# Attention with its projections in four column groups and its transposes in row tiles, ahead of a GRU

## The chip, the core and the metric

The kernel runs on one core of a Trainium2 chip. The core has five engines with instruction queues of their own: TensorE (PE, with its weight loads, PEld), VectorE (DVE), ScalarE (ACT), GpSimd (POOL) and SyncE (SP), which here only issues DMAs. The metric is the device time in microseconds (us) of one execution. All data are fp32.

## The reference

For each of 16 batches, with x of 256 tokens by 512 features and a condition vector `cond`:

```python
scale, shift = split(cond @ W_emb + b_emb)
xn = rms_norm(x, g_norm) * (1 + scale) + shift
q, k, v = split(xn @ W_qkv)              # 16 heads of 32
q, k = rms_norm(q, g_q), rms_norm(k, g_k)   # over the 32 of a head
o = softmax(q @ k.T * 32**-0.5) @ v
x = x + o + o @ W_out
h = cond                                    # GRU, 256 steps in sequence over t
gi, gh = x[:, t] @ W_ih + b_ih, h @ W_hh + b_hh    # each split into r, z, n
r, z = sigmoid(gi_r + gh_r), sigmoid(gi_z + gh_z)
n = tanh(gi_n + r * gh_n)
h = (1 - z) * n + z * h;  out[:, t] = x[:, t] + h
```

## The kernel before

The program has two halves. The first does the attention of all batches and keeps the heads' outputs on chip in `oT`. The second runs the GRU over 256 time steps; between its steps it computes the output projection and the input product of later steps. Only the first half and what leads into it is touched by the edit. The GRU's `product` (L648), which the edit leaves alone, already writes four column groups: four matmuls with 32 stationary columns each, to partitions 0, 32, 64 and 96 of one PSUM bank.

The loop over the attention (L579 to L586) has four slots per batch, one for each group of four heads. Slot g of batch b does two kinds of work. One is the attention of the group: logits (L300), the negated row maxima (`maxima`), exponentials with their sums (`exps`), and the division by the sums on GpSimd (`normalize`). The group before it, `prev`, goes on at the same time: its attention matrix is transposed (`turn`), copied out of PSUM (`put_turned`), multiplied with v (`weigh`) and copied to `oT` (`put_weighed`). The other kind prepares batch m = b + 1: its q, k and v projections for both halves n of the tokens (`project`), the norm of q and k (`Stats`, `norm_qk`), their transposes (`turn_qk`) and the copies of these to `qT` and `kT`. The x of later batches is normed too: batch b + 3's is squared in slot 2 and scaled in slot 3, and in slot 0 the x of batch b + 2 is transposed (`turn_x`) and written with scale and shift to `xnT` (`put_x`).

A projection of 128 tokens to 512 outputs takes four steps, one for each 128 features k; a step is one fp32 matmul of 128 stationary columns and 512 moving columns, which the machine runs as two issues. The 24 steps of a batch are spread over the four slots. Where a projection is begun in one slot and ended later, its accumulator stays in PSUM. There are eight PSUM banks: lg0 to lg3 hold the logits and, once the exponentials are done, the transposes of the group before; A, X, Y and Z go from one use to the next.

Transposes go through TensorE: the data are the stationary operand and the identity is the moving one. Those of x, q and k take a whole 128x128 block in one issue. The attention's, in `turn`, take two row tiles of 64 partitions, R and QR in the code, each of which writes its own bank, so that `put_turned` puts the interleaved halves back.

The order on TensorE, VectorE, ScalarE and GpSimd is the order in which the code is written (`manual_schedule`); there is no planner. An engine waits for the operand of its next instruction and everything behind it waits too. The lines of the profile that matter are L242 (projection), L310 (logits), L361 (transposes of the attention), L282 and L221 (transposes of q, k and of x), L385 (weighing), L325 (maxima), L331 (exponentials), L233 and L231 (copies of x), L287 and L292 (copies of q and k), L375 (copies of the attention), L262 (copy of v), L268 (norm of q and k).

The last batch has four short slots (`slot_last`), without work for a next batch. Ahead of the loop, the x of the first batches and all of batch 0's projections are done.

Of the kernel before, what the change touches and what calls it, by code (L numbers as in the profile page):

```python
# [9 lines left out]
AF = mybir.ActivationFunctionType  # L10
ALU = mybir.AluOpType
AX = mybir.AxisListType
PSUM = bass.MemoryType.PSUM

P = 128
# [4 lines left out]
def kernel(  # L20
# [17 lines left out]
    nc = tc.nc  # L38
# [3 lines left out]
    KC = D // P  # L42
# [119 lines left out]
    def tile_ps(name, bank, shape=(P, D)):  # L162
        pool = ps if len(bank) == 1 else ps_lg
        return pool.tile(list(shape), F32, tag=bank, name=name)
# [48 lines left out]
        if 0 < b and b + 2 < B:  # L213
            load_x(b + 2)

    def turn_x(b, half, bank):
        tp = tile_ps(f"tpx_{b}_{half}", bank, (P, 2, T))
        for cc in range(2):
            c = 2 * half + cc
            for n in range(NT):  # L220
                nc.tensor.transpose(  # L221
                    tp[:, cc, n * P : (n + 1) * P], batches[b].xs[:, n, c * P : (c + 1) * P], ident
                )
        return tp

    def put_x(b, half, tp, engine=nc.vector):
        for cc in range(2):
            c = 2 * half + cc
            a, s = ada_a[:, c, b : b + 1], ada_s[:, c, b : b + 1]
            if engine is nc.scalar:  # L230
                nc.scalar.activation(batches[b].xnT[:, c, :], tp[:, cc, :], AF.Identity, bias=s, scale=a)  # L231
            else:
                nc.vector.tensor_scalar(  # L233
                    batches[b].xnT[:, c, :], tp[:, cc, :], a, s, ALU.mult, ALU.add
                )

    def project(b, n, s, ks, a):

        if isinstance(a, str):
            a = tile_ps(f"qkv_{b}_{n}_{s}", a)  # L240
        for k in ks:
            nc.tensor.matmul(  # L242
                a,
                batches[b].xnT[:, k, n * P : (n + 1) * P],
                wq[:, k, s * D : (s + 1) * D],
                start=(k == 0),
                stop=(k == KC - 1),
            )
        return a

    def square(b, n, s, a):
# [23 lines left out]
        return out  # L275

    def turn_qk(b, n, normed, banks):
        tps = []
        for s in range(2):
            tp = tile_ps(f"tpqk_{b}_{n}_{s}", banks[s], (P, NG, P))  # L280
            for c in range(NG):
                nc.tensor.transpose(tp[:, c, :], normed[s][:, c * P : (c + 1) * P], ident)  # L282
            tps.append(tp)
        return tps

    def put_q(n, tps):
        nc.vector.tensor_scalar(qT[:, :, n * P : (n + 1) * P], tps[0], gq_col, None, ALU.mult)  # L287

    def put_k(n, tps, engine=nc.scalar):
        dst = kT[:, :, n * P : (n + 1) * P]  # L290
        if engine is nc.scalar:
            nc.scalar.activation(dst, tps[1], AF.Copy, scale=gk_col)  # L292
        else:
            nc.vector.tensor_scalar(dst, tps[1], gk_col, None, ALU.mult)


    class Group:
# [24 lines left out]

    def maxima(w, heads):
        for i in heads:
            nc.vector.tensor_reduce(w.neg[:, i, :], w.lg[i], AX.X, ALU.max, negate=True)  # L325

    def exps(w, heads):
        for i in heads:
# [8 lines left out]
    def normalize(w, heads=range(HG), engine=nc.gpsimd):  # L337
        r = slice(heads[0], heads[-1] + 1)
        nc.vector.reciprocal(w.rden[:, r, :], w.den[:, r, :])  # L339
        for i in heads:  # L340
            for n in range(NT):
# [2 lines left out]
                    ALU.mult, ALU.mult,  # L344
                )

    R, QR = 2, P // 2

    def turn(w, banks=("lg0", "lg1", "lg2", "lg3")):

        if w is None:
            return
        w.tp = [tile_ps(f"tpa_{w.b}_{w.g}_{i}", banks[i], (P, R, NT, NT, QR)) for i in range(HG)]
        for i in range(HG):
            for n in range(NT):
                for k in range(NT):
                    for r in range(R):
                        q = slice(QR * r, QR * r + QR)  # L360
                        nc.tensor.transpose(  # L361
                            w.tp[i // R * R + r][:, i % R, k, n, :],
                            w.attn[i][q, n, k * P : (k + 1) * P],
                            ident[q, q],
                        )
        w.attnT = p1.tile([P, HG, NT, T], F32, tag="attnT", name=f"attnT_{w.b}_{w.g}")

    def put_turned(w, engines):

        if w is None:  # L370
            return
        for i, e in enumerate(engines):
            h, r = i // R * R, i % R
            dst = w.attnT[:, h : h + R].rearrange("p h k (n r c) -> p h k n r c", n=NT, r=R)[:, :, :, :, r]
            (nc.scalar.copy if e == "a" else nc.vector.tensor_copy)(dst, w.tp[i])  # L375

    def weigh(w, bank):
        if w is None:
            return
        v = batches[w.b].v  # L380
        w.o = tile_ps(f"o_{w.b}_{w.g}", bank, (P, T))
        for k in range(NT):
            for i in range(HG):
                h = w.g * HG + i
                nc.tensor.matmul(  # L385
                    w.o[i * DH : (i + 1) * DH, :],
                    v[:, k, h * DH : (h + 1) * DH],
                    w.attnT[:, i, k, :],
                    start=(k == 0),
                    stop=(k == NT - 1),  # L390
                )
# [20 lines left out]
    def slot0(b, w, prev, st):  # L412
        m = b + 1
        if b == 0:
            rstd = batches[2].rs.second()
        maxima(w, range(HG))
        if b == 0:
            norm_apply(2, rstd)
        project(b, 1, 2, range(1 if b == 0 else 2, KC), st.v1)
        if b == 0:  # L420
            st.q = project(m, 0, 0, (0,), "A")
        if b + 2 < B:
            tpx = [turn_x(b + 2, half, "YZ"[half]) for half in range(2)]
        if b == 0:
            project(m, 0, 0, range(1, KC), st.q)
        else:
            st.q = project(m, 0, 0, (0, 1), "A")
        exps(w, range(HG))
        if b + 2 < B:
            for half in range(2):  # L430
                put_x(b + 2, half, tpx[half])
        put_v(b, 1, st.v1)
        turn(prev)
        put_turned(prev, "vava")
        if b > 0:
            project(m, 0, 0, (2, 3), st.q)
        normalize(w)
        weigh(prev, "Z")
        st.s0 = Stats(m, 0)
        st.sq = st.s0.square(0, st.q)  # L440
        put_weighed(prev)

    def slot1(b, w, prev, st):
        m = b + 1
        k = project(m, 0, 1, range(KC), "Y")
        st.q1 = project(m, 1, 0, (0, 1), "Z")
        maxima(w, range(HG))
        exps(w, range(HG))
        st.s0.add(0, st.sq)
        st.s0.add(1, st.s0.square(1, k))  # L450
        st.s0.rs.first()
        turn(prev)
        put_turned(prev, "vava")
        project(m, 1, 0, (2, 3), st.q1)
        rstd = st.s0.rs.second()
        weigh(prev, "X")
        normalize(w)
        st.qk0 = norm_qk(m, 0, (st.q, k), rstd)
        st.s1 = Stats(m, 1)
        st.sq = st.s1.square(0, st.q1)  # L460
        put_weighed(prev)
# [26 lines left out]
    def slot3(b, w, prev, st):  # L488
        m = b + 1
        last = m == B - 1  # L490
        tq0 = turn_qk(m, 0, st.qk0, "ZA")
        project(m, 0, 2, (2, 3), st.v0)
        st.v1 = project(m, 1, 2, (0, 1) if last else (0,), "X")
        maxima(w, range(HG))
        if b + 3 < B:
            rstd = batches[b + 3].rs.second()
        put_q(0, tq0)
        if b + 3 < B:
            norm_apply(b + 3, rstd)
        exps(w, range(HG))  # L500
        put_v(m, 0, st.v0)
        put_k(0, tq0)
        turn(prev)
        put_turned(prev, "vava")
        tq1 = turn_qk(m, 1, st.qk1, "ZA")
        project(m, 1, 2, (2, 3) if last else (1,), st.v1)
        put_q(1, tq1)
        put_k(1, tq1)
        normalize(w)
        weigh(prev, "Y")  # L510
        if last:
            put_v(m, 1, st.v1)
        put_weighed(prev)
# [17 lines left out]
    with tc.manual_schedule(engines=ORDERED):  # L531
# [9 lines left out]
        wih = wpool.tile([P, KC, 3 * D], F32, tag="w_a", name="wih")  # L541
        for k in range(KC):
            nc.sync.dma_start(wih[:, k, :], w_ih[k * P : (k + 1) * P, :])
        for half in range(2):
            put_x(0, half, turn_x(0, half, "AX"[half]))
        q = project(0, 0, 0, range(KC), "Y")
        k = project(0, 0, 1, range(KC), "Z")
        s0 = Stats(0, 0)
# [9 lines left out]
        norm_apply(1, batches[1].rs.second())  # L558
        k = project(0, 1, 1, range(KC), "X")
        tq = turn_qk(0, 0, qk, ("lg0", "lg1"))  # L560
        tpx = [turn_x(1, half, f"lg{2 + half}") for half in range(2)]
        v = project(0, 0, 2, range(KC), "Y")
        s1.add(1, s1.square(1, k))
        s1.rs.first()
        put_q(0, tq)
        put_k(0, tq, nc.vector)
        qk = norm_qk(0, 1, (q, k), s1.rs.second())
        for half in range(2):
            put_x(1, half, tpx[half], nc.scalar)
        norm_first(2)  # L570
        batches[2].rs.first()
        tq = turn_qk(0, 1, qk, "ZA")
        st.v1 = project(0, 1, 2, (0,), "X")
        put_q(1, tq)
        put_k(1, tq)
        put_v(0, 0, v)

        prev = None
# [286 lines left out]
```

## Time and profile before

| | us |
|---|---|
| median of three runs (1822.04 to 1822.92) | 1822.74 |
| profiled execution | 1822.2 |
| its span, first to last instruction | 1820.4 |
| TensorE busy in matmuls | 1754.8 |
| VectorE, ScalarE, GpSimd busy | 1114.5, 815.0, 316.2 |
| projection matmuls (L242) busy, 768 issues | 362.6 |
| transposes of attention, of q and k, of x busy | 88.3, 34.9, 17.7 |

A line of the timeline gives the start in us from the span's start, the length in us, the engine, the line of the kernel, the operation, out<-in by the program's names, the rows*columns of the array that the instruction uses, the shape, and the count of merged instructions; an idle time in brackets is that of the engine ahead of the instruction, with what ended it. A line of the groups gives busy time, mean ns of one instruction, and idle time ahead of it with what ended it. Since matmuls are pipelined, their lengths overlap; from one group of matmuls to the next the difference of the starts is what counts.

### The profile page before, as it was taken

To read this page: it belongs to the slowest core of one execution; us is meant where nothing else is said; L and a number is where in the kernel's file an instruction comes from. 1 tells how busy PE (TensorE), PEld (TensorE's weight loads), DVE (VectorE), ACT (ScalarE), POOL (GpSimd) and SP (SyncE) were. 2 spreads that over 40 slices of the span, in tenths; PEclk is the share of its full clock that TensorE was granted. 3 is DMA by queue.
4 is the path that set the end of the run, shared out by engine and by line. 5 is a ranking of instruction groups with operands and counts; after the bars stand their busy time and mean duration, and the time that the engine had idled before them with its cause. 6 is when DMAs were issued, how large, how long until landed. Compare 5 with 4: busy or idle time off the path is not lost.

```text
span 1820.4 us, 86417 instructions
## 1 busy us (share of the span) xinstructions
PE 1754.8 (96%) x38066; PEld 1237.9 (68%) x38066; DVE 1114.5 (61%) x3611; ACT 815.0 (45%) x2723; POOL 316.2 (17%) x769
## 2 busy tenths in 40 slices
PE   7999999999999889999999999999999999999975
PEld 3555555555555447887887887888888888888865
DVE  4666666666766635566566566566566565665555
ACT  3677777777777633333333333333333333333322
POOL 0434333433433320000000000000000000000000
PEclk9999999999999989999999999999999999999999
DMA  7200000000000110001101101100110100000000
GB/s 260 54 13 13 13 24 13 13 14 13 13 2 1 71 25 10 15 17 24 18 16 22 21 16 19 23 16 15 22 21 15 21 16 10 11 15 10 10 15 15
DMA packets 146200, 43.37 MB, mean 24 GB/s; under 512 B 137899, under 2 KB 138031, under 8 KB 145823
## 3 DMA queue, kind: packets, MB, share of 16 engines
q1 hardware_dynamic: 145287, 36.72, 8.8%
q8 instruction: 299, 4.90, 1.1%
q10 hardware_dynamic: 536, 1.12, 0.2%
q14 instruction: 78, 0.64, 0.1%
HBM read 29.41 MB, written 8.39 MB: 21 GB/s over the span
## 4 chain that ended last, share of the span: by engine, by line
PE 85%; DVE 6%; ACT 6%; issue 2%; DMA 1%; POOL 0%; ACTq 0%; DVEq 0%; POOLq 0%
PE gi L651 17%; PE qkv L242 14%; PE gr L713 13%; PE gn L713 12%; PE gz L713 11%; PE o L651 6%; ACT attn L331 5%; PE lg L310 4%; PE o L385 4%; PE tpa L361 3%; DVE neg L325 2%; DVE tr L725 1%; PE tpqk L282 1%; PE tpx L221 1%; DVE h L816 0%
## 5 line engine op out<-in xcount | busy, mean ns | idle before, releaser
L651 PE MATMUL gi<-xT,wih 128*32 128x256 f32 x6144 | 364.7, 379 | 0.0
L242 PE MATMUL qkv<-wq,xnT 128*128 128x512 f32 x768 | 362.6, 606 | 0.0
L342 POOL TENSOR_SCALAR attn<-attn,rden 128x256 f32<-128x256 f32 x508 | 233.5, 483 | 422.2 <-DVE rden L339 331.9
L713 PE MATMUL gr<-whh,h 128*16 128x128 f32 x8160 | 272.2, 274 | 25.1 <-DVE h L817 23.7
L713 PEld LDWEIGHTS gr<-whh,h 128*16 128x16 f32 x8160 | 200.5, 96 | 108.6 <-DVE h L817 108.6
L331 ACT ACTIVATE attn<-lg,neg 128x256 f32<-128x256 f32 x512 | 234.8, 485 | 82.0 <-DVE neg L325 47.8
L713 PE MATMUL gz<-whh,h 128*16 128x128 f32 x8160 | 269.5, 273 | 0.0
L713 PE MATMUL gn<-whh,h 128*16 128x128 f32 x8160 | 269.5, 273 | 0.0
L819 POOL TENSOR_TENSOR y<-xT,h 128x64 f32<-128x64 f32 x255 | 81.9, 321 | 1071.6 <-DVE h L817 1034.5
L651 PEld LDWEIGHTS gi<-xT,wih 128*32 128x32 f32 x6144 | 195.9, 110 | 100.9
L788 ACT ACTIVATE r<-r 128x64 f32<-128x64 f32 x256 | 65.7, 257 | 380.4 <-DVE r L787 380.4
L325 DVE TENSOR_REDUCE neg<-lg 128x2 f32<-128x512 f32 x256 | 158.9, 683 | 117.6 <-PE lg L310 116.5
L242 PEld LDWEIGHTS qkv<-wq,xnT 128*128 128x128 f32 x768 | 135.4, 190 | 137.5 <-issue 129.3
L725 DVE STREAM_TRANSPOSE tr<-gr 128x128 f32<-128x128 f32 x256 | 81.1, 317 | 237.1 <-PE gr L713 237.1
L713 PEld LDWEIGHTS gn<-whh,h 128*16 128x16 f32 x8160 | 224.7, 97 | 0.0
L713 PEld LDWEIGHTS gz<-whh,h 128*16 128x16 f32 x8160 | 224.7, 97 | 0.0
L695 ACT ACTIVATE gi<-gi,cols 128x256 f32<-128x256 f32 x192 | 91.2, 475 | 163.9 <-PE gi L651 163.9
L725 DVE STREAM_TRANSPOSE tr<-gn 128x128 f32<-128x128 f32 x256 | 81.1, 317 | 76.0 <-PE gn L713 76.0
L651 PE MATMUL o<-oT,wo 128*32 128x256 f32 x2048 | 121.7, 379 | 0.7 <-ACT oT L396 0.7
L361 PEld LDWEIGHTS tpa<-ident,attn 64*128 64x128 f32 x2048 | 75.1, 142 | 61.8 <-issue 45.1
L331 ACT ACTIVATION_READ_ACCUMULATOR attn<-lg,neg 128x1 f32 x512 | 111.0, 217 | 0.0
L794 ACT ACTIVATE n<-n 128x64 f32<-128x64 f32 x256 | 65.5, 256 | 98.5 <-DVE n L793 98.5
(98 smaller groups left out, 1720.8 us busy)
## 6 DMA issues: line engine op xcount, KB each, us to landing
x<-in_x_dram SPq DMA_DIRECT2D x16, 512.0 KB, 3.6
xin<-in_x_dram SPq DMA_DIRECT2D x256, 32.0 KB, 2.6
out_dram<-osb SPq DMA_DIRECT2D x248, 32.0 KB, 3.2
wq<-in_L_cond_W_qkv_dram SPq DMA_DIRECT2D x12, 256.0 KB, 4.2
wih<-in_L_cond_W_ih_dram SPq DMA_DIRECT2D x4, 768.0 KB, 10.9
whh<-in_L_cond_W_hh_dram SPq DMA_DIRECT2D x4, 768.0 KB, 5.7
we<-in_L_cond_W_emb_dram SPq DMA_DIRECT2D x2, 512.0 KB
we<-in_L_cond_W_emb_dram ACTq DMA_DIRECT2D x2, 512.0 KB, 6.5
```

What stands on the lines that cost most here:

```text
L242: nc.tensor.matmul(a, batches[b].xnT[:, k, n * P : (n + 1) * P], wq[:, k, s * D : (s + 1) * D], start=(k == 0), stop=(k == KC - 1),)
L310: nc.tensor.matmul(w.lg[i][:, n, :], qT[r, g, n * P : (n + 1) * P], kT[r, g, :], start=True, stop=True,)
L325: nc.vector.tensor_reduce(w.neg[:, i, :], w.lg[i], AX.X, ALU.max, negate=True)
L331: nc.scalar.activation(a[:, n, :], w.lg[i][:, n, :], AF.Exp, bias=w.neg[:, i, n : n + 1], accum_out=w.den[:, i, n : n + 1],)
L342: engine.tensor_scalar(w.attn[i][:, n, :], w.attn[i][:, n, :], w.rden[:, i, n : n + 1], 1.0, ALU.mult, ALU.mult,)
L361: nc.tensor.transpose(w.tp[i // R * R + r][:, i % R, k, n, :], w.attn[i][q, n, k * P : (k + 1) * P], ident[q, q],)
L385: nc.tensor.matmul(w.o[i * DH : (i + 1) * DH, :], v[:, k, h * DH : (h + 1) * DH], w.attnT[:, i, k, :], start=(k == 0), stop=(k == NT - 1),)
L651: nc.tensor.matmul(acc[32 * j : 32 * j + 32, :], w[:, k, m * P + 32 * j : m * P + 32 * j + 32], rhs, start=(k == 0), stop=(k == KC - 1),)
L695: nc.scalar.activation(gis[grp][:, m].rearrange("p t b -> p (t b)"), acc["i"], AF.Identity, bias=bcols[:, m : m + 1],)
L713: nc.tensor.matmul(gates[g][32 * j : 32 * j + B, :], hT[:, k, :], whh[:, k, g * D : (g + 1) * D].rearrange("p (q j c) -> p j q c", q=KC, c ...
L725: nc.vector.transpose(tr.rearrange("p q b -> p (q b)"), gates[g])
L819: (nc.gpsimd if t + 1 < T else nc.vector).tensor_tensor(y[:, :, tl * B : (tl + 1) * B], xTs[grp][:, :, ti, :], h, ALU.add)
```

## The change

- `project` writes four column groups: each step is four matmuls with 32 tokens as stationary columns, to the partitions 32j to 32j + 31 of the bank, all with the same 512 moving columns.
- `turn_block` takes over the two row tiles of `turn`, and `turn_x` and `turn_qk` use it as well. A tile of x or of q and k now holds one half r (64 of each 128 tokens), in one bank for each r; x's two banks hold all four feature chunks, and those of q and k hold both.
- `put_x` copies one half r with eight instructions in all of 128x128 for a batch (four of 128x256 before). `put_qk` takes the place of `put_q` and `put_k`: VectorE copies half 0 of q and of k, ScalarE half 1 of both, each 128x256 (before, VectorE copied q and ScalarE k, each 128x512).
- `maxima` reduces the first head in two instructions, one for each half n of the tokens; the other heads as before.
- The order in the slots: transposes of x stand right ahead of `turn` in slot 0; in slot 3 those of q and k stand right ahead of it and right behind it, and the projection steps ahead of and behind these. Slot 0 now has one step of batch b's v and, of batch m, four of q and one of k; slot 1 has seven steps, slot 2 six, slot 3 five. The weighing of slot 0 goes to bank X in place of Z. In slot 3 the norm of x is issued on VectorE ahead of the copies of q and k.
- Ahead of the loop the same helpers are used, with the copies of x of batch 0 dealt to VectorE and ScalarE.

```diff
+    R, QR = 2, P // 2
+    def turn_block(dst, src):
+        for r in range(R):
+            q = slice(QR * r, QR * r + QR)
+            nc.tensor.transpose(dst[r], src[q], ident[q, q])
+    def turn_x(b, banks):
+        tps = [tile_ps(f"tpx_{b}_{r}", banks[r], (P, KC, NT, QR)) for r in range(R)]
+        for c in range(KC):
             for n in range(NT):
-                nc.tensor.transpose(
-                    tp[:, cc, n * P : (n + 1) * P], batches[b].xs[:, n, c * P : (c + 1) * P], ident
+                turn_block(
+                    [tp[:, c, n, :] for tp in tps], batches[b].xs[:, n, c * P : (c + 1) * P]
                 )
+    def put_x(b, r, tps, chunks=range(KC), engine=nc.vector):
+        for c in chunks:
+            dst = batches[b].xnT[:, c, :].rearrange("p (n r q) -> p n r q", n=NT, r=R)[:, :, r]
...
         for k in ks:
-            nc.tensor.matmul(
-                a,
-                batches[b].xnT[:, k, n * P : (n + 1) * P],
-                wq[:, k, s * D : (s + 1) * D],
+            for j in range(4):
+                nc.tensor.matmul(
+                    a[32 * j : 32 * j + 32, :],
+                    batches[b].xnT[:, k, n * P + 32 * j : n * P + 32 * j + 32],
+                    wq[:, k, s * D : (s + 1) * D],
...
+        tps = [tile_ps(f"tpqk_{b}_{n}_{r}", banks[r], (P, 2, NG, QR)) for r in range(R)]
         for s in range(2):
             for c in range(NG):
-                nc.tensor.transpose(tp[:, c, :], normed[s][:, c * P : (c + 1) * P], ident)
+                turn_block([tp[:, s, c, :] for tp in tps], normed[s][:, c * P : (c + 1) * P])
+    def put_qk(n, r, tps, engine):
+        for s, (dst, g) in enumerate(((qT, gq_col), (kT, gk_col))):
+            dst = dst[:, :, n * P + QR * r : n * P + QR * r + QR]
+            if engine is nc.scalar:
+                nc.scalar.activation(dst, tps[r][:, s], AF.Copy, scale=g)
+            else:
+                nc.vector.tensor_scalar(dst, tps[r][:, s], g, None, ALU.mult)
...
         for i in heads:
-            nc.vector.tensor_reduce(w.neg[:, i, :], w.lg[i], AX.X, ALU.max, negate=True)
+            for n in (slice(0, 1), slice(1, 2)) if i == 0 else (slice(0, 2),):
+                nc.vector.tensor_reduce(
+                    w.neg[:, i, n], w.lg[i][:, n, :], AX.X, ALU.max, negate=True
+                )
...
@@ slot0 @@
+        project(b, 1, 2, range(1, KC) if b == 0 else (3,), st.v1)
+        before = 1 if b == 0 else 3
+        st.q = project(m, 0, 0, range(before), "A")
+        tpx = turn_x(b + 2, "YZ") if b + 2 < B else None
         exps(w, range(HG))
         put_v(b, 1, st.v1)
         turn(prev)
+        if tpx:
+            put_x(b + 2, 0, tpx)
         put_turned(prev, "vava")
+        if tpx:
+            put_x(b + 2, 1, tpx)
+        project(m, 0, 0, range(before, KC), st.q)
+        st.k = project(m, 0, 1, (0,), "Y")
         normalize(w)
-        weigh(prev, "Z")
+        weigh(prev, "X")
...
@@ slot1 @@
-        k = project(m, 0, 1, range(KC), "Y")
+        k = project(m, 0, 1, range(1, KC), st.k)
...
@@ slot3 @@
+        project(m, 0, 2, (2, 3), st.v0)
+        st.v1 = project(m, 1, 2, (0, 1), "X")
         tq0 = turn_qk(m, 0, st.qk0, "ZA")
-        project(m, 0, 2, (2, 3), st.v0)
-        st.v1 = project(m, 1, 2, (0, 1) if last else (0,), "X")
         maxima(w, range(HG))
...
-        put_q(0, tq0)
...
         put_v(m, 0, st.v0)
-        put_k(0, tq0)
+        put_qk(0, 0, tq0, nc.vector)
+        put_qk(0, 1, tq0, nc.scalar)
         turn(prev)
         put_turned(prev, "vava")
         tq1 = turn_qk(m, 1, st.qk1, "ZA")
-        project(m, 1, 2, (2, 3) if last else (1,), st.v1)
-        put_q(1, tq1)
-        put_k(1, tq1)
+        project(m, 1, 2, (2, 3) if last else (2,), st.v1)
+        put_qk(1, 0, tq1, nc.vector)
+        put_qk(1, 1, tq1, nc.scalar)
```

More of the change, by code (lines that the diff above doesn't have):

```diff
@@ L214, in norm_apply @@
             load_x(b + 2)
[L216 to L219, printed above, removed]
+    R, QR = 2, P // 2
[6 more added lines that the diff above has]
+        for c in range(KC):
             for n in range(NT):
-                nc.tensor.transpose(
-                    tp[:, cc, n * P : (n + 1) * P], batches[b].xs[:, n, c * P : (c + 1) * P], ident
-                )
[L224 to L228, printed above, removed]
+                turn_block(
+                    [tp[:, c, n, :] for tp in tps], batches[b].xs[:, n, c * P : (c + 1) * P]
+                )
+        return tps
+    def put_x(b, r, tps, chunks=range(KC), engine=nc.vector):
+        for c in chunks:
             a, s = ada_a[:, c, b : b + 1], ada_s[:, c, b : b + 1]
+            dst = batches[b].xnT[:, c, :].rearrange("p (n r q) -> p n r q", n=NT, r=R)[:, :, r]
             if engine is nc.scalar:
-                nc.scalar.activation(batches[b].xnT[:, c, :], tp[:, cc, :], AF.Identity, bias=s, scale=a)
+                nc.scalar.activation(dst, tps[r][:, c], AF.Identity, bias=s, scale=a)
             else:
-                nc.vector.tensor_scalar(
-                    batches[b].xnT[:, c, :], tp[:, cc, :], a, s, ALU.mult, ALU.add
-                )
+                nc.vector.tensor_scalar(dst, tps[r][:, c], a, s, ALU.mult, ALU.add)
     def project(b, n, s, ks, a):
@@ L241, in project @@
         for k in ks:
-            nc.tensor.matmul(
-                a,
-                batches[b].xnT[:, k, n * P : (n + 1) * P],
-                wq[:, k, s * D : (s + 1) * D],
-                start=(k == 0),
-                stop=(k == KC - 1),
-            )
+            for j in range(4):
[3 more added lines that the diff above has]
+                    wq[:, k, s * D : (s + 1) * D],
+                    start=(k == 0),
+                    stop=(k == KC - 1),
+                )
         return a
@@ L277, in turn_qk @@
     def turn_qk(b, n, normed, banks):
-        tps = []
+        tps = [tile_ps(f"tpqk_{b}_{n}_{r}", banks[r], (P, 2, NG, QR)) for r in range(R)]
         for s in range(2):
-            tp = tile_ps(f"tpqk_{b}_{n}_{s}", banks[s], (P, NG, P))
             for c in range(NG):
-                nc.tensor.transpose(tp[:, c, :], normed[s][:, c * P : (c + 1) * P], ident)
-            tps.append(tp)
-        return tps
[L286 to L294, printed above, removed]
+                turn_block([tp[:, s, c, :] for tp in tps], normed[s][:, c * P : (c + 1) * P])
+        return tps
+    def put_qk(n, r, tps, engine):
[5 more added lines that the diff above has]
+                nc.vector.tensor_scalar(dst, tps[r][:, s], g, None, ALU.mult)
     class Group:
@@ L324, in maxima @@
         for i in heads:
-            nc.vector.tensor_reduce(w.neg[:, i, :], w.lg[i], AX.X, ALU.max, negate=True)
+            for n in (slice(0, 1), slice(1, 2)) if i == 0 else (slice(0, 2),):
+                nc.vector.tensor_reduce(
+                    w.neg[:, i, n], w.lg[i][:, n, :], AX.X, ALU.max, negate=True
+                )
     def exps(w, heads):
@@ L345, in normalize @@
                 )
-    R, QR = 2, P // 2
     def turn(w, banks=("lg0", "lg1", "lg2", "lg3")):
@@ L358, in turn @@
                 for k in range(NT):
[L359 to L365, printed above, removed]
+                    turn_block(
+                        [w.tp[i // R * R + r][:, i % R, k, n, :] for r in range(R)],
+                        w.attn[i][:, n, k * P : (k + 1) * P],
+                    )
         w.attnT = p1.tile([P, HG, NT, T], F32, tag="attnT", name=f"attnT_{w.b}_{w.g}")
@@ L418, in slot0 @@
             norm_apply(2, rstd)
[L419 to L427, printed above, removed]
+        project(b, 1, 2, range(1, KC) if b == 0 else (3,), st.v1)
+        before = 1 if b == 0 else 3
+        st.q = project(m, 0, 0, range(before), "A")
+        tpx = turn_x(b + 2, "YZ") if b + 2 < B else None
         exps(w, range(HG))
-        if b + 2 < B:
-            for half in range(2):
-                put_x(b + 2, half, tpx[half])
         put_v(b, 1, st.v1)
         turn(prev)
+        if tpx:
+            put_x(b + 2, 0, tpx)
         put_turned(prev, "vava")
-        if b > 0:
-            project(m, 0, 0, (2, 3), st.q)
+        if tpx:
+            put_x(b + 2, 1, tpx)
+        project(m, 0, 0, range(before, KC), st.q)
+        st.k = project(m, 0, 1, (0,), "Y")
         normalize(w)
-        weigh(prev, "Z")
+        weigh(prev, "X")
         st.s0 = Stats(m, 0)
@@ L543 @@
             nc.sync.dma_start(wih[:, k, :], w_ih[k * P : (k + 1) * P, :])
-        for half in range(2):
-            put_x(0, half, turn_x(0, half, "AX"[half]))
+        tpx = turn_x(0, "AX")
+        for c in range(KC):
+            put_x(0, 0, tpx, (c,))
+            put_x(0, 1, tpx, (c,), nc.scalar)
         q = project(0, 0, 0, range(KC), "Y")
@@ L560 @@
         tq = turn_qk(0, 0, qk, ("lg0", "lg1"))
-        tpx = [turn_x(1, half, f"lg{2 + half}") for half in range(2)]
+        tpx = turn_x(1, ("lg2", "lg3"))
         v = project(0, 0, 2, range(KC), "Y")
@@ L564 @@
         s1.rs.first()
-        put_q(0, tq)
-        put_k(0, tq, nc.vector)
+        put_qk(0, 0, tq, nc.vector)
+        put_qk(0, 1, tq, nc.scalar)
         qk = norm_qk(0, 1, (q, k), s1.rs.second())
-        for half in range(2):
-            put_x(1, half, tpx[half], nc.scalar)
+        for r in range(R):
+            put_x(1, r, tpx, engine=nc.scalar)
         norm_first(2)
@@ L573 @@
         st.v1 = project(0, 1, 2, (0,), "X")
-        put_q(1, tq)
-        put_k(1, tq)
+        put_qk(1, 0, tq, nc.vector)
+        put_qk(1, 1, tq, nc.scalar)
         put_v(0, 0, v)
```

## The prediction

> **What bounds the kernel now.** I read the page's chain first, then the order in time of TensorE alone over one batch of the attention loop, then the groups of instructions by shape. The chain that ended last is TensorE almost throughout:
>
> ```profile
> PE 85%; DVE 6%; ACT 6%; issue 2%; DMA 1%; POOL 0%; ACTq 0%; DVEq 0%; POOLq 0%
> ```
>
> The loop's slots start with the logits (L310). Their first starts, 16 issues apart, run from 40.71 us (batch 0) to 622.50 us (batch 15): 15 batches, the ordinary one 38.74 us, its slots 9.65, 10.49, 9.32 and 9.29. After that come four short slots, and from 661.7 us the GRU, which the edit doesn't touch. TensorE's timeline, one slot 3 and one slot 1 (start, length to the modelled end, line, out<-in, tile rows*columns, shape, count):
>
> ```profile
> 302.50 1.15 PE L310 MATMUL lg<-kT,qT 32*128 32x256 f32 x16
> 303.58 1.09 PE L282 MATMUL tpqk<-ident,qkn 128*128 128x128 f32 x8
> 304.51 2.74 PE L242 MATMUL qkv<-wq,xnT 128*128 128x512 f32 x6
> 307.18 0.77 PE L361 MATMUL tpa<-ident,attn 64*128 64x64 f32 x17
> 308.26 0.71 PE L361 MATMUL tpa<-ident,attn 64*128 64x64 f32 x15 [0.31 <-ACT attn L331]
> 308.90 1.09 PE L282 MATMUL tpqk<-ident,qkn 128*128 128x128 f32 x8
> 309.83 1.02 PE L242 MATMUL qkv<-wq,xnT 128*128 128x512 f32 x2
> 310.78 1.07 PE L385 MATMUL o<-attnT,v 128*32 128x256 f32 x16
> 311.78 1.15 PE L310 MATMUL lg<-kT,qT 32*128 32x256 f32 x16
> ...
> 321.43 1.15 PE L310 MATMUL lg<-kT,qT 32*128 32x256 f32 x16
> 322.51 5.42 PE L242 MATMUL qkv<-wq,xnT 128*128 128x512 f32 x12
> 327.86 1.22 PE L361 MATMUL tpa<-ident,attn 64*128 64x64 f32 x32
> 329.00 1.98 PE L242 MATMUL qkv<-wq,xnT 128*128 128x512 f32 x4
> 330.92 1.07 PE L385 MATMUL o<-attnT,v 128*32 128x256 f32 x16
> ```
>
> Every start follows the one before it closely: the loop is bound by TensorE's streaming, by its changes between tile shapes, and by one wait, in slot 3 (and alike in slot 2), where the attention's transposes stop for the exponentials (0.54 us between where 17 issues end streaming and 308.26). A projection step is two issues; their weight loads stand 0.43 us apart, so a step is 0.86. The groups of four that run side by side have their price in the GRU's input product:
>
> ```profile
> 668.62 20.90 PE L651 MATMUL gi<-xT,wih 128*32 128x256 f32 x384
> ...
> 689.34 0.40 PE L703 MATMUL gn<-ident 128*32 128x128 f32 x8
> ```
>
> 384 issues in 20.72 us are 96 quads of 0.216 us for 256 columns; 512 columns are 0.43. Rows for the copies that get smaller:
>
> ```profile
> L233 DVE TENSOR_SCALAR xnT<-tpx,ada_a,ada_s 128x256 f32<-128x256 f32 x60 | 28.4, 534 | 1.8 <-PE tpx L221 1.8
> ...
> L231 ACT ACTIVATE xnT<-tpx,ada_s,ada_a 128x256 f32<-128x256 f32 x4 | 1.9, 558 | 0.0
> ```
>
> **What the Trainium skill says.** TensorEngine Tiling (Array Packing), Tiling Modes, says that changing the tiling mode, not just the tile, drains TensorE. The trace agrees: the projections' 12 issues need 12 x 0.43 = 5.16 and the next shape starts after 5.35; four quads of logits or weighing need 0.862 and take 1.08 and 1.00. The same page, Restrictions, says that column tiling disables the transpose mode for fp32; the edit puts transposes in row tiles alone, as L361 does now. Its Gotcha 1 wants different row tiles in different PSUM banks; the edit gives each its own. TensorE: Matmul & The Clock Gate, Part 3, measures only 2.38x for three column tiles at 512 columns; the 0.216 us quads here are full overlap at 256, so no loss shows, and 512 is not in this trace.
>
> **The change, part by part.** Over pure streaming, slot 1 pays logits to projection 0.22, projection to transposes 0.19, transposes to projection 0.12 (1.14 less 32 issues of 0.032), projection to weighing 0.20, weighing to logits 0.14: 0.87.
>
> *Projections in column groups.* A step becomes 8 issues in two quads: 0.86, unchanged. Issue rate: 8 loads and 8 matmuls in 0.86 us, which the GRU's input product sustains. What goes is projection to weighing, since both are then 128*32: 0.20 per slot, 0.80 per batch (bounds: 0.10, if half of it is a weight load that stays exposed, to 0.25, if a step's first load of 32 columns, 110 ns, also shortens the change ahead of it against 190 ns for 128).
>
> *Transposes of x, q, k in row tiles.* A 128x128 block costs 0.109 now (x: 8 from 314.68 to 315.55) or 0.116 (8 in 0.93), and as two 64-row issues 2 x 0.032 = 0.064. 24 blocks per batch: 24 x 0.045 = 1.08. They join the attention's transposes, so no shape change is added; slot 3 loses one pair of changes, about 0.1.
>
> *Steps dealt 6, 7, 6, 5.* Now they are 6, 8, 6, 4: the sum of 24 stays, 0.86 moves from slot 1 to slot 3.
>
> Streaming and changes after, with 0.67 left for changes: slot 0, 5.16 + 1.72 + 1.02 + 0.51 + 0.67 = 9.08; slot 1, 6.02 + 1.72 + 1.02 + 0.67 = 9.43; slot 2, 8.57; slot 3, 4.30 + 1.72 + 1.02 + 1.02 + 0.67 = 8.73. Sum 35.8, with no wait.
>
> *First maximum in two halves.* The L325 reduce takes 0.683 for 512 elements (0.60 apart) and starts when the whole head is written, 1.16 after the logits start; exponentials start 0.79 later and come 0.45 apart, so they end at 1.95 + 8 x 0.45 = 5.6. The first half of head 0 is written 0.43 sooner, and its reduce, unmeasured, is between 0.35 (half) and 0.683; I take 0.47, which is 0.683 less 256 elements at 0.83 ns (VectorE's 128x256 copy takes 0.534, its 128x512 copy of q, L287, 0.747). Exponentials then start near 1.16 - 0.43 + 0.47 + 0.1 = 1.3 and, with 0.1 more ahead of head 1, end near 5.1, 0.5 sooner. VectorE pays about 0.2. Thus the waits of 0.54 (slot 3) and 0.51 (slot 2) for the exponentials go: the transposes of heads 2 and 3 come at 5.2 in slot 2 and later elsewhere.
>
> *What is late next.* Slot 3: the second q/k transposes need both banks Z and A back, from VectorE and ScalarE. VectorE reaches the maxima late, as now (1.16 after the logits), because it first ends the norm of q and k of slot 2: from the last sum of squares to there it takes 3.4 (300.11 to 303.50), from near 6.4 in a slot that now lasts 8.6. I get 1.3, the exponentials from 1.3 + 0.47 + 0.1, the last issued at 5.0, the copy of v at 5.5, then ScalarE's two pieces of 128x256 (0.558 each by L231, 0.45 apart; the old 128x512 by L292 took 0.755) end near 6.9. TensorE is through the attention's transposes at 1.08 + 3.44 + 0.19 + 0.51 + 1.02 = 6.24 and waits 0.65 (bounds 0 to 1.1). Behind it on TensorE stand one step and the weighing. Slot 0: the x copies become eight of 128x128, priced between 0.27 (half) and 0.534, I take 0.43, and 0.35 apart (now 0.452) by the same slope: 1.5 us ahead of the attention's copies on VectorE, from 5.4 to 6.9, the two copies after them to 8.1, where the weighing wants to start: 0.1 wait (0 to 0.5). The other four copies follow before the reciprocal, which makes GpSimd's normalize start some 2 us later; it takes 3.67 and is wanted only 5.5 us into slot 1. The q and k copies cost VectorE 0.36 and ScalarE 0.3 more per batch, under TensorE's work apart from the wait named. The norm of x moves ahead of q's copy on VectorE, so the load of x on SP's queue comes earlier; the landing is 3.6 us and nobody waits.
>
> Batch: 35.8 + 0.75 = 36.55, a gain of 2.2; 15 batches 33. The four last slots have no projections, and their chain runs logits, maxima, exponentials, copy, weighing: 0.5 each, 2.0. Ahead of the loop, 32 blocks in row tiles gain 1.4 less about four more changes of shape at 0.2: 0.6. Total 35.6. The profiled execution took 1822.2, of which the span is 1820.4; it becomes 1784.8, the execution 1786.6. The median of the runs lay 0.5 above it: **1787 us**.
>
> **The rivals.** *Waits take the gain back.* The first half may not release VectorE early (its wait might be for the whole tile), and the copies may cost their upper bounds: slots 2 and 3 then wait about 0.5 each for the exponentials again, slot 3's wait for bank A grows by 0.3, and slot 0 loses 0.3. Batch about 37.7: gain 1.0 x 15 + 1 = 16, 1807; with half of that, 1798. For it: slot 3 has both engines on the path. Against: the interleaved halves of the attention's copies run on two engines at once now (328.60 and 328.87), so halves are told apart.
>
> *The change to the weighing keeps its price,* because the 0.20 is a wait for the attention's copies and not a drain. Then 0.8 x 15 = 12 less: 1799. Against: at 330.92 the copies had been done for 1.0 us.
>
> *Slower: four column groups of 512 columns do not overlap fully.* Attention has 384 steps, 768 quads. The gain of 36 is eaten at 0.047 us per quad, a quad of 0.477 instead of 0.430. At the skill's 2.38 of three the quad is 0.54 and the loss 85: 1822 - 36 + 85 = 1872. For it: that page. Against it: the 256-column quads at 0.216.
>
> *Nothing changes:* a chain through ScalarE and VectorE sets the slots. The shortest, exponentials' end 5.1, two heads' transposes 0.7, a copy 0.7, weighing 1.0, is 7.5 us, below every slot; small chance.
>
> **How the numbers follow.** Chances: the forecast 0.70 (own range 1779 to 1796: all waits gone 35.8 per batch gives 1776, the bad ends of some of them the other), waits 0.15, price kept 0.06, slower 0.06, nothing 0.03. The range to 1803 takes in the third case and the lesser half of the second. A difference below 0.2% (3.6 us) can't be told from none: faster 0.90, same 0.03, slower 0.07.
>
> **What would show it.** The projection's group reads 128*32 with 3072 issues, four of them per 0.43 us; projection to weighing loses its 0.2; x, q, k read 64*128, two issues per 0.064; batches 36.5 apart; the stop inside the attention's transposes gone, and a new one before the second q/k transposes in slot 3, released by ScalarE. A quad above 0.44, exponentials that start later than 1.5 us after the logits in slots 0 to 2, or waits of over 1.5 us per batch would make it wrong.

## The result, and the profile after

The changed kernel takes 1810.2 us (1809.8 to 1811.1, four runs) against 1822.4 of the kernel before on the same chip: a ratio of 0.9933, 95% interval 0.9916 to 0.9951. It is faster, by 12 us and not by 35. The profiled execution took 1810.6, its span 1808.8.

The chain that ended last has lost a little of TensorE and has won some of ScalarE:

```profile
PE 84%; ACT 8%; DVE 5%; issue 2%; DMA 1%; POOL 0%; ACTq 0%; DVEq 0%
```

TensorE's timeline of a slot 3, and of a slot 1 with the slot 2 behind it (columns as explained in the section on time and profile before):

```profile
302.92 0.71 PE L224 MATMUL tpqk<-ident,qkn 64*128 64x64 f32 x16
303.47 1.36 PE L224 MATMUL tpa<-ident,attn 64*128 64x64 f32 x32
304.69 0.24 PE L224 MATMUL tpqk<-ident,qkn 64*128 64x64 f32 x1
305.33 0.71 PE L224 MATMUL tpqk<-ident,qkn 64*128 64x64 f32 x15 [0.40 <-ACT kT L297]
305.97 1.07 PE L250 MATMUL qkv<-wq,xnT 128*32 128x512 f32 x8
306.85 1.05 PE L388 MATMUL o<-attnT,v 128*32 128x256 f32 x16
307.83 1.15 PE L315 MATMUL lg<-kT,qT 32*128 32x256 f32 x16
...
317.02 1.15 PE L315 MATMUL lg<-kT,qT 32*128 32x256 f32 x16
318.10 4.50 PE L250 MATMUL qkv<-wq,xnT 128*32 128x512 f32 x40
322.53 1.22 PE L224 MATMUL tpa<-ident,attn 64*128 64x64 f32 x32
323.68 1.92 PE L250 MATMUL qkv<-wq,xnT 128*32 128x512 f32 x16
325.42 1.28 PE L388 MATMUL o<-attnT,v 128*32 128x256 f32 x16
326.64 1.15 PE L315 MATMUL lg<-kT,qT 32*128 32x256 f32 x16
327.71 3.64 PE L250 MATMUL qkv<-wq,xnT 128*32 128x512 f32 x32
331.28 0.77 PE L224 MATMUL tpa<-ident,attn 64*128 64x64 f32 x17
332.48 0.71 PE L224 MATMUL tpa<-ident,attn 64*128 64x64 f32 x15 [0.42 <-ACT attn L340]
333.12 1.92 PE L250 MATMUL qkv<-wq,xnT 128*32 128x512 f32 x16
```

Three things are as foreseen. The weighing starts 1.74 us after the two steps of projection (x16) ahead of it and not 1.92, so the cost of a change of shape there is gone. The transposes of q and k take 0.55 for eight blocks (302.92 to 303.47), not 0.93. And the second q/k transposes stop after one issue, from 304.69 to 305.33, for ScalarE. One is not: in slot 2 the attention's transposes still stop for the exponentials, from the end of 17 issues to 332.48, some 0.66 us, where the prediction had no stop. In slot 3, where the attention's transposes now come later (5.2 us after the logits, 4.7 before), they run through.

VectorE and ScalarE in that slot 2, whose logits start at 326.64, show why:

```profile
327.80 2.55 DVE L332 TENSOR_REDUCE neg<-lg 128x1 f32<-128x256 f32 x5 [0.50 <-PE lg L315]
```
```profile
328.67 0.47 ACT L340 ACTIVATE attn<-lg,neg 128x256 f32<-128x256 f32 x1 [1.31 <-DVE neg L332]
```

A slot 2 of the kernel before, whose logits start at 331.92:

```profile
333.08 2.48 DVE L325 TENSOR_REDUCE neg<-lg 128x2 f32<-128x512 f32 x4 [1.32 <-PE lg L310]
```
```profile
333.87 0.47 ACT L331 ACTIVATE attn<-lg,neg 128x256 f32<-128x256 f32 x1 [1.22 <-DVE neg L325]
```
```profile
336.63 0.77 PE L361 MATMUL tpa<-ident,attn 64*128 64x64 f32 x17
337.68 0.71 PE L361 MATMUL tpa<-ident,attn 64*128 64x64 f32 x15 [0.28 <-ACT attn L331]
```

The maxima start 1.16 us after the logits, as they did before the change, and the first exponential 2.03 after them (2.04 in slots 1 and 3); it was 1.95. More than 1.5 was one of the prediction's signs of being wrong. The reduce of half a head takes 0.42 us (group of that shape: busy, mean ns | idle ahead of it):

```profile
L332 DVE TENSOR_REDUCE neg<-lg 128x1 f32<-128x256 f32 x128 | 48.4, 420 | 70.0 <-PE lg L315 69.6
```

The spans differ by 11.6 us, and the starts of the logits show where: from the span's start to the first slot it is 2.5 longer (43.20 against 40.71); the 15 batches are 14.8 shorter (566.98 against 581.79), the ordinary one 37.69 against 38.74; from the last batch to the end it is 0.7 longer. The slots of an ordinary batch, in us, are:

| slot | before | forecast | after |
|---|---|---|---|
| 0 | 9.65 | 9.2 | 9.20 |
| 1 | 10.49 | 9.43 | 9.61 |
| 2 | 9.32 | 8.6 | 9.32 |
| 3 | 9.29 | 9.4 | 9.56 |

Ahead of the loop, the first logits wait for ScalarE:

```profile
43.20 1.15 PE L315 MATMUL lg<-kT,qT 32*128 32x256 f32 x16 [1.70 <-ACT kT L297]
```

### The profile page after: what moved, and what is told of

Read it like the earlier page. It is cut to its first block, busy times and chain, and to the rows that moved or that the text cites. A ratio compares the mean times of both kernels' runs of the same rounds, so it can differ in the third digit from the quotient of the medians.

```text
span 1808.8 us, 92032 instructions
## 1 busy us (share of the span) xinstructions
PE 1736.3 (96%) x40754; PEld 1192.8 (66%) x40754; DVE 1131.9 (63%) x3762; ACT 819.8 (45%) x2764; POOL 314.4 (17%) x769
## 4 chain that ended last, share of the span: by engine, by line
PE 84%; ACT 8%; DVE 5%; issue 2%; DMA 1%; POOL 0%; ACTq 0%; DVEq 0%
PE gi L652 17%; PE gr L714 13%; PE qkv L250 13%; PE gn L714 12%; PE gz L714 11%; ACT attn L340 6%; PE o L652 6%; PE lg L315 4%; PE o L388 4%; PE tpa L224 3%; DVE neg L332 1%; DVE tr L726 1%; PE tpqk L224 1%; PE tpx L224 1%; ACT z L798 0%
## 5 line engine op out<-in xcount | busy, mean ns | idle before, releaser
L250 PE MATMUL qkv<-wq,xnT 128*32 128x512 f32 x3072 | 356.4, 598 | 0.5 <-DVE xnT L242 0.5
L250 PEld LDWEIGHTS qkv<-wq,xnT 128*32 128x32 f32 x3072 | 88.5, 110 | 181.0 <-issue 166.9
L332 DVE TENSOR_REDUCE neg<-lg 128x2 f32<-128x512 f32 (+1 forms) x320 | 163.1, 576 | 70.0 <-PE lg L315 69.6
```

The lines of the kernel that those rows point to most:

```text
L250: nc.tensor.matmul(a[32 * j : 32 * j + 32, :], batches[b].xnT[:, k, n * P + 32 * j : n * P + 32 * j + 32], wq[:, k, s * D : (s + 1) * D], ...
L332: nc.vector.tensor_reduce(w.neg[:, i, n], w.lg[i][:, n, :], AX.X, ALU.max, negate=True)
```

## The experiments

Theory A, formed on these lines: the first half of head 0 is not handed to VectorE before its whole tile is written, and its maximum not to ScalarE before the second half's; so the cut starts nothing sooner, and the exponentials, a little late, still hold up slot 2. Rival B: the exponentials are not what holds them; the copies on VectorE and ScalarE are, cut small or queued differently. Rival C: the column groups are not worth what the drain says, or cost something. Each ratio is to the kernel before on the same chip: 1821.9 us for the first four experiments, 1822.1 for the other three, 1822.4 for the changed kernel itself. Batches and slots are from the traces, one of each kernel, in which the ordinary batches agree within 0.03 us.

**The maximum in one instruction again.**

```diff
-            for n in (slice(0, 1), slice(1, 2)) if i == 0 else (slice(0, 2),):
+            for n in (slice(0, 2),):
```

> The changed kernel (1810.2 us, batch 37.69 us) with the first head's maximum in one instruction again. Theory A (the first half is not released before its whole tile is written, so the cut only adds time): exponentials start 1.95 us after the logits in place of 2.04, the wait inside slot 2's transposes shrinks by about 0.1, batch 37.5 to 37.6, 1806 to 1810 us. Rival B (the cut does start the exponentials sooner and something else eats it): exponentials later by 0.4 or more, batch 38.2, about 1818 us.

Measured: 1805.1 us (1804.5 to 1806.6), ratio 0.9907 (0.9892 to 0.9921). Exponentials start 1.95 after the logits, and the batch is 37.35, 0.34 shorter: slots 9.11, 9.52, 9.24 and 9.47, each by 0.08 or 0.09. So the cut is a loss of some 5 us, and rival B's form of it falls. The size is more than expected, since I had counted the gain in slot 2 alone: with the cut, all four slots are longer by about what it delays the exponentials.

**The first half in a bank of its own.** Three edits: the tile, its users, and the order of a norm that frees bank Y.

```diff
-    def logits(b, g):
+    def logits(b, g, spare=None):
+        w.first = tile_ps(f"lgf_{b}_{g}", spare, (P, T)) if spare else w.lg[0][:, 0, :]
+        w.half = lambda i, n: w.first if (i, n) == (0, 0) else w.lg[i][:, n, :]
...
-                w = logits(b, g)
+                w = logits(b, g, ("Z", "Z", "Y", None)[g] if b + 1 < B else None)
...
-        st.qk0 = norm_qk(m, 0, (st.q, k), rstd)
+        st.qk0 = norm_qk(m, 0, (st.q, k), rstd, (1, 0))
```

The logits, the maximum and the exponential of head 0 use `w.half(0, n)` in place of a slice of `w.lg[0]`; no instruction is added.

> The changed kernel with the first half of head 0's logits in a PSUM bank of its own in slots 0, 1 and 2 (Z, Z, Y; slot 3 and the last four slots stay), and the norm of k ahead of that of q in slot 1 so that Y is back in time. Theory A: the first maximum starts near 0.75 us after the logits, the exponentials near 1.3 in place of 2.04, the wait of 0.66 us inside slot 2's transposes goes, slot 2 falls from 9.32 to 8.6 to 8.8, slot 1 from 9.61 to about 9.45, batch near 36.9, 1797 to 1801 us. Rival B (slot 2 is held by the copies and the sums of squares on VectorE and ScalarE, not by the start of the exponentials): exponentials earlier, slot 2 above 9.1, above 1806 us.

Measured: 1797.4 us (1796.9 to 1802.6), ratio 0.9870 (0.9855 to 0.9885). VectorE and ScalarE in a slot 2 whose logits start at 321.01:

```profile
321.75 0.42 DVE L334 TENSOR_REDUCE neg<-lgf 128x1 f32<-128x256 f32 x1 [0.52 <-PE lgf L317]
```
```profile
322.26 0.47 ACT L343 ACTIVATE attn<-lgf,neg 128x256 f32<-128x256 f32 x1 [0.51 <-DVE neg L334]
```

and TensorE in it:

```profile
322.09 3.64 PE L250 MATMUL qkv<-wq,xnT 128*32 128x512 f32 x32
325.66 1.24 PE L224 MATMUL tpa<-ident,attn 64*128 64x64 f32 x32
326.83 1.92 PE L250 MATMUL qkv<-wq,xnT 128*32 128x512 f32 x16
328.57 1.17 PE L391 MATMUL o<-attnT,v 128*32 128x256 f32 x16
329.67 1.15 PE L317 MATMUL lg<-kT,qT 32*128 32x256 f32 x16
```

The first maximum starts 0.74 after the logits and the first exponential 1.25, the 32 transposes run without a stop, and slot 2 is 8.66, as slot 1 is 9.37. The same instructions, with another place for one half, give what the prediction had expected of the cut; so the shared place was the obstacle. The built program, in which the waits are written, agrees. With head 0 in one tile the first half's matmul signals nobody and the first reduce carries the wait for the whole head; and this reduce signals nobody either, so ScalarE waits for the second one. With two tiles each half has its own signals. The edit gives the half another tile and another bank at once, so which of the two counts is not shown. The two norms that changed places were not tried alone; but VectorE is idle for 0.5 us between them and the first maximum in both kernels, so they do not set its start. Slot 3, without a bank of its own, stays at 9.54. Slot 0 grew from 9.20 to 9.38: the logits of slot 1 now want bank Z, which the second four copies of x give back only then (wait for VectorE of 0.21 at 311.64). The batch is 36.95.

**Batch 1's x copied by two engines.**

```diff
-            put_x(1, r, tpx, engine=nc.scalar)
+            put_x(1, r, tpx, engine=(nc.vector, nc.scalar)[r])
```

> The changed kernel with the copies of batch 1's x, ahead of the loop, dealt to VectorE (half 0) and ScalarE (half 1) in place of all eight on ScalarE. Theory A (the logits of the first slot wait 1.70 us for ScalarE's copy of k, behind those eight copies of 0.36): four of them gone from ScalarE, the loop's first logits come 1.3 to 1.5 us sooner, 1808.7 to 1809 us. Rival (the start is late for the loads and the clock alone): no change, 1810.2 us.

Measured: 1806.7 us (1806.4 to 1806.9), ratio 0.9914 (0.9900 to 0.9929), 2 us better than expected. The first logits:

```profile
42.51 1.15 PE L315 MATMUL lg<-kT,qT 32*128 32x256 f32 x16 [0.31 <-DVE u_x L185]
```

From the first transposes of q and k to these logits it is 6.74 us, and it was 8.14 in the changed kernel and 7.01 before. That is the 1.4 expected, and ScalarE's queue is shown to be the cause of it. The other 2 us are not in the lines that the edit touches: from the last batch on, where nothing differs, this execution took 1195.6 us and the changed kernel's 1198.7, while its first projection came 0.45 later. The last section returns to that.

**q and k ahead of v on ScalarE in slot 3.**

```diff
-        put_v(m, 0, st.v0)
         put_qk(0, 0, tq0, nc.vector)
         put_qk(0, 1, tq0, nc.scalar)
+        put_v(m, 0, st.v0)
```

> The changed kernel with ScalarE's copies of the first q and k halves of slot 3 ahead of its copy of v. Theory A (the second transposes of q and k wait 0.63 us for bank A, which ScalarE reads last, behind the copy of v): the wait falls by 0.45, slot 3 from 9.56 to about 9.1, batch 37.25, 1803 to 1805 us. Rival (what ScalarE does later then holds the weighing or the next logits): slot 3 stays above 9.4, above 1808 us.

Measured: 1804.9 us (1801.5 to 1806.1), ratio 0.9907 (0.9890 to 0.9923); slot 3 is 9.07 and the batch 37.20. TensorE in slot 3:

```profile
300.78 1.36 PE L224 MATMUL tpa<-ident,attn 64*128 64x64 f32 x32
302.00 0.86 PE L224 MATMUL tpqk<-ident,qkn 64*128 64x64 f32 x16
```

The 16 issues at 302.00 are no longer cut in two. The wait for bank A was real, was the one foreseen, and could be had back by an exchange of two lines.

**Projections over the whole array again.**

```diff
-            for j in range(4):
-                nc.tensor.matmul(
-                    a[32 * j : 32 * j + 32, :],
-                    batches[b].xnT[:, k, n * P + 32 * j : n * P + 32 * j + 32],
+            nc.tensor.matmul(
+                a,
+                batches[b].xnT[:, k, n * P : (n + 1) * P],
```

> The changed kernel (1810.2 us, batch 37.69 us) with each projection step as one matmul of 128 stationary columns again; all else stays. Theory A (a change of tile shape between projection and weighing costs 0.2 us of draining): each slot gains such a change, slots 0 and 3 grow by 0.2, slots 1 and 2 by 0.1 to 0.2 since the weighing waits there a little anyway, batch 38.2 to 38.4, 1818 to 1821 us. Rival C (the 0.2 is not a drain, or the column groups of 512 columns cost something of their own): no change or faster, at most 1811 us.

Measured: 1817.1 us (1815.9 to 1817.7), ratio 0.9972 (0.9962 to 0.9983), a little below the range expected. The batch is 38.19: slots 9.41, 9.63, 9.40 and 9.76, more by 0.21, 0.02, 0.08 and 0.20. Slots 0 and 3 pay the change of shape in full; in slots 1 and 2 the weighing waits for copies in the changed kernel (in slot 1 it takes 1.22 to the next logits there, and 1.00 here). TensorE in a slot 0:

```profile
317.31 1.98 PE L249 MATMUL qkv<-wq,xnT 128*128 128x512 f32 x4
319.22 1.07 PE L387 MATMUL o<-attnT,v 128*32 128x256 f32 x16
```

The weighing starts 1.91 behind the projection in place of 1.74. So the column groups are worth 0.50 per batch in this kernel, 7 us, and of the 0.80 forecast 0.3 met other waits.

**The column groups alone, on the kernel before.** The same edit the other way, in `before`.

> The kernel before (batch 38.74 us) with nothing but the projections in four column groups. Theory A: slots 1 and 2 lose one change of shape, but in slots 0 and 3 the transposes of x, q and k, still over the whole array, now stand between projections of another shape and add one or two: batch 38.4 to 39.1, 1818 to 1828 us. Rival C (column groups are worth 0.2 per slot whatever stands beside them): 38.0, 1811 us; rival C the other way (they cost): above 1830 us.

Measured: 1814.7 us (1812.9 to 1816.7), ratio 0.9962 (0.9949 to 0.9974). The batch is 38.43, in the range expected, with slots of 9.67, 10.23, 9.24 and 9.28; the time is lower than expected. The profiled execution has a span 5.5 us shorter than that of the kernel before, and 3.1 of it lie behind the loop again (1194.8 us from the last batch on, for 1197.9), where nothing was changed. TensorE in slot 0:

```profile
312.93 1.92 PE L243 MATMUL qkv<-wq,xnT 128*32 128x512 f32 x16
314.78 1.09 PE L221 MATMUL tpx<-ident,xs 128*128 128x128 f32 x8
315.80 1.92 PE L243 MATMUL qkv<-wq,xnT 128*32 128x512 f32 x16
317.66 1.22 PE L362 MATMUL tpa<-ident,attn 64*128 64x64 f32 x32
```

Around whole-array transposes the column groups pay: 4.73 us from 312.93 to 317.66, where the kernel before took 4.51, and with the 0.17 saved ahead of the weighing slot 0 comes out level. In slot 1, where nothing of that kind stands, 0.26 is left. So both sides of the account, a change of shape saved and one made dearer, show in one kernel, and neither form of rival C holds.

**What helped, joined.** This run has the bank of its own in slots 0 and 2 only, the maximum cut only there, q and k ahead of v, and x of batch 1 on two engines. Against the changed kernel it is the three edits above, with:

```diff
+            for n in (slice(0, 1), slice(1, 2)) if i == 0 and w.own else (slice(0, 2),):
...
+                w = logits(b, g, ("Z", None, "Y", None)[g] if b + 1 < B else None)
```

where `w.own` is true if the group has a bank of its own.

> The changed kernel with what the first four runs showed put together: the first half of head 0's logits in a bank of its own in slots 0 and 2 only (Z, Y), where its maximum is cut; the maximum whole in all other slots; the q and k copies of slot 3 ahead of the copy of v; batch 1's x copied by both engines. Theory A: slots near 9.0, 9.5, 8.7 and 9.0, batch 36.2, 15 x 1.5 = 22 us less than the changed kernel and 1 to 3 more ahead of the loop, 1784 to 1788 us. Rival B (the waits only move on to VectorE's and ScalarE's copies): batch above 36.8, above 1795 us.

Measured: 1788.9 us (1786.6 to 1789.4), ratio 0.9816 (0.9803 to 0.9830): it beats both kernels, and is 1 to 5 us above what I had expected. The batch is 36.48: slots 9.09, 9.74, 8.63 and 9.01. Slot 1 is the one that misses, by 0.24; between its weighing and the logits of slot 2 there are 1.35 us (315.96 to 317.31) where a slot without a wait has 0.97 to 1.0. These logits write bank Y, which the norm of k, issued on VectorE at 316.47 and 0.69 long, reads until just ahead of that; some 0.15 of it is the weighing's own wait for copies. So the waits move on in part, as rival B has it, but they take 0.3 us and leave 1.2.

## Why the prediction was wrong

The span came out 24.0 us above the forecast of 1784.8. Of these 18.2 lie in the 15 batches, 3.1 ahead of them and 2.7 behind.

**The step that failed is "First maximum in two halves".** It had the exponentials start 1.3 us after the logits and end near 5.1, and took the waits of slots 2 and 3 away for that. They start at 2.03, and slot 2 keeps its wait, 0.66 for 0.51 before; the wait of slot 3 went, but because its transposes come later. The size of a half's reduce was nearly right (0.42 for 0.47); its start was not. Given its own bank in three of the slots the batch falls by 0.74, and left whole it falls by 0.34: the cut as it was made bought nothing and cost 5 us, and with the bank it saves 0.40 per batch against the maximum left whole. The prediction had this as a rival, "waits take the gain back", with 1807 us and a batch of 37.7 for it and a chance of 0.15. The batch is met, but in part by luck: slot 0 lost nothing, and the wait for bank A did not grow by 0.3. The prediction put this rival aside because the interleaved halves of the attention's copies run on two engines at once. That was the wrong evidence: there, two engines write parts of one tile in SBUF, the on-chip memory of the operands; here one would read part of a PSUM tile that another is still writing. The right evidence was in the trace of the kernel before, ahead of the loop, where x of batch 0 is transposed into two tiles of four transposes each:

```profile
16.61 2.15 PE L221 MATMUL tpx<-ident,xs 128*128 128x128 f32 x8 [1.64 <-DVE xs L208]
```
```profile
17.94 1.90 DVE L233 TENSOR_SCALAR xnT<-tpx,ada_a,ada_s 128x256 f32<-128x256 f32 x4 [0.99 <-PE tpx L221]
```

The first copy reads only what the first two transposes write, and by the trace the second of these ends at 17.48. VectorE, idle, starts the copy at 17.94, just behind the end of the fourth at 17.90: it waits for the whole tile, and in the built program only the fourth signals. Short of that, the bound from both sides that the reduce's length was given should have been given to its start.

**The last four slots** were to gain 0.5 each for the same reason. The first three grew by 0.2 in sum, about as much as they differ by between the changed kernel and the run with batch 1's x on two engines, where their instructions are the same; whether the cut costs anything there is not shown.

**Ahead of the loop** the forecast of 0.6 gained was a sum over TensorE alone, and 2.5 was lost. ScalarE's eight copies of x take 2.9 us where four took 1.9, with a q and a k piece ahead of them and another pair behind, and the logits wait 1.70: from the first transposes of q and k on, 1.1 is lost by that. The other 1.4 is there when these transposes start (35.06 against 33.70), nearly all of it before the first projection (19.87 against 18.55). The edit has little part in that: from the first transpose of x to the first projection it is 1.91 for 1.94. Of the delay 0.6 was there when the rows of constants were transposed (14.20 against 13.56; from 13.5 to 14.6 in the nine profiles). Another 0.7 came in the projection of the condition, whose last matmul starts 1.49 after those rows in every other profile, that of the column groups alone on the kernel before among them, and 0.82 in the kernel before. There its groups of four matmuls start 0.21 us apart, and in the changed kernel 0.41; the profile of the kernel before records TensorE's full clock there, from 11.0 to 14.4. So some 1.3 of the 3.1 come from how the two executions began.

**Right, with their sizes.** A step in four column groups is 0.86 us: 10 quads (groups of four issues that run side by side) in slot 1 take 4.43 with the change of shape behind them. The Trainium skill's mere 2.38x for three column tiles at 512 columns (TensorE: Matmul & The Clock Gate, Part 3) does not show as a loss here: 3072 issues go at the same pace as the whole array's 768, and rival "slower" is out.

The Trainium skill's drain at a change of mode (TensorEngine Tiling (Array Packing), Tiling Modes) agrees with the 0.18 saved ahead of the weighing (1.92 to 1.74), 0.20 in the forecast. It was worth 0.50 of the 0.80 per batch (rival "keeps its price" is out as well), the rest being hidden behind the weighing's wait for copies in slots 1 and 2, which the forecast had not charged.

The transposes of x, q and k go at 0.069 us per block for 0.064. Slot 0 came to 9.20 for 9.2. The wait before the second q/k transposes in slot 3 is 0.64 for 0.65, with the place, the bank and the engine foreseen.

**What is left of the loop's shortfall of 1.14 per batch:** 0.75 in slot 2, of which 0.66 goes when the exponentials start early; 0.18 in slot 1, where the weighing waits for ScalarE's copies, which follow the exponentials, the square and the logarithm, and which goes with an early start too; 0.18 in slot 3, of which 0.09 goes with the cut; 0.02 in slot 0.

## What to carry to other kernels

To split an instruction so that its first half starts sooner, make sure that its producer hands over the halves one by one: whether parts of a tile are kept apart in waits must be seen for that memory and that pair of engines, in the trace or in the built program. In PSUM, a tile in a bank of its own did it here. A change of tile shape on TensorE, once removed, is worth its 0.2 us only where the instruction behind it is not waiting for something else, so charge each saving to a slot and ask who is next. Outside the loop, walk the queue of every engine, not just that of the bound one: copies cut into more pieces cost nothing in slot 0, beside a busy TensorE (9.20 as forecast), and cost 1.1 us ahead of the loop, where TensorE waits for them.

## What the runs showed of the hardware

TensorE's granted clock, as the profiles record it, was full without a break from between 21.2 and 23.8 us after the start to the last batch. It was half for stretches of 3.4 or 6.8 us in that batch's sparse slots and just behind them, 4 to 38 us after its first logits and at different places in each execution, and again in the last 3 to 6.5 us.

From the last batch's first logits to the end, the nine profiles took 1194.8 to 1198.7 us, with the same instructions but for the cut of the maximum, worth some 0.3 there by an estimate from the 0.08 to 0.09 per slot above. The half clock does not explain these 4 us: the execution with the most of it there, that of the column groups alone (23.9 us), was the shortest. Most of the difference lies in the GRU at full clock: from its first input product to the end it is 1148.2 us in that execution and 1152.0 in the changed kernel's. The cause is open. It may go with the kernel and not with the execution alone: the four runs of the changed kernel (1809.8 to 1811.1) and the four with batch 1's x on two engines (1806.4 to 1806.9) do not overlap, while the kernel before took 1822.4 and 1821.9 beside them. So differences below 4 us between kernels are read here from the batches, which repeat within 0.03 us.

Four column groups of 512 columns overlap without loss, 0.43 us for four issues (ten quads in 4.43, change of shape included), as they do at 256. The kernel before had not shown that.
